# Slots' stage of a triangle and Fourier layer: x arrives with channels on partitions from the first stage's transposes, the factors' product moves to GpSimd, and the loads ahead of the triangle go

## Chip, cores and metric

The kernel runs on 1 core of one Trainium2 chip. The metric is the device time of one execution in microseconds, the median of several runs. All data is float32. The engines are TensorE (PE, with its weight loads shown as PEld), VectorE (DVE), ScalarE (ACT), GpSimd (POOL) and SyncE (SP, which only issues DMAs here).

## What is computed

x has the shape (1, 512, 512, 64): 512 rows, 512 columns, 64 channels. Two layers follow each other, each with a group normalisation in front and a residual sum behind. The reference, cut to what matters:

```python
# layer 0, on xn = _ln(_gn(x), norm_w, norm_b)
left  = (xn @ left_w  + left_b)  * mask * sigmoid(xn @ lgate_w + lgate_b)
right = (xn @ right_w + right_b) * mask * sigmoid(xn @ rgate_w + rgate_b)
out_gate = sigmoid(xn @ ogate_w + ogate_b)
out = einsum('bkjd,bkid->bijd', left, right)
x = x + (_ln(out, onorm_w, onorm_b) @ out_w + out_b) * out_gate
# layer 1: 12 x 12 Fourier modes of _gn(x), mixed over channels, and back
x = x + irfft_of_modes(einsum('bcmn,comn->bomn', fft2(_gn(x))[:12, :12], w))
```

`mask` is the outer product of a 0/1 vector of 512 entries with itself. Where it is 0 the row or column gives nothing to `left`, `right` and the einsum.

## The kernel before

With at most 256 (`K`) valid entries in the mask the branch `compact` runs, as it does with these inputs. Rows of x are ordered by rank, the valid ones first, so that the first two blocks of 128 ranks (`r` = 0 and 1) hold all valid rows; a *slot* is a valid column. Blocks 2 and 3 hold the other rows. The stages follow each other:

1. **Reading x** (L683 to L782). For each of 16 tiles `jc` of 32 columns, `fetch_tile` issues four indirect gathers of 1 MB on POOL's queue (blocks 0 and 1 into the two halves of `xg`, blocks 2 and 3 into two `yg`), two tiles ahead. PE transposes pairs of columns (128 rows by 2 x 64 channels) into banks `x_ps` of four transposes, six banks in turn (L768), and VectorE takes `bn_stats` of each bank (L769). `keep` copies the columns that are slots out of `xg` into the resident buffer `xc`: one copy for each of the 32 columns, 128 rows by 2 blocks by 64 channels, into a place whose number is a register value. Columns that are no slot go into a spare place behind the 256. ScalarE copies columns 0 to 21 (`SHARE`), GpSimd 22 to 31 (L746); the registers are filled by `slots_of` (L653) with loads of up to 16 values. `scale_weights`, `keep_weights`, `widen` and `keep_wide` put small ScalarE steps between the tiles.
2. **Scale and shift**: `group_norm_affine` joins the statistics into `ab1`.
3. **The slots' stage** (L799 to L956), 64 groups `q` of four slots, order written by hand. Per group: PE transposes the four slots so that channels lie on partitions (`turn_x`, L822; the first six groups ahead, in banks that are still free); ScalarE applies scale and shift and writes the result over `xc` (`channels`, L832); PE subtracts the mean over channels (`centered`, L843), ScalarE squares, VectorE sums (L944). For four groups at a time nine small VectorE steps (`rsqrt_steps`) make 1/sqrt; `spread` transposes these factors on PE, copies them (L862), writes them to `rs_d` in DRAM and reads them back as a broadcast to 64 partitions (L863, L869, both on POOL's queue). VectorE multiplies (`normed`, L876), PE projects twice ("gates", "sides", L882), ScalarE takes the sigmoids (L914), VectorE adds the bias and multiplies (L939), and SP stores `left_d` and `right_d`. Normalising runs 13 groups (`lead`) ahead of projecting. `early`, at the groups in `turns`, gathers x for a later stage into parts of `xc` whose slots are done, on POOL's queue. In the last four groups `load_sides` (L796) already loads seven eighths of the first four channels' `left_d` and `right_d`.
4. **The triangle** (L966 to L1016): 64 channels, each with transposes of the two sides, a product, and a store of `tri_d`.
5. The rest: the outer normalisation, gate and residual, statistics, Fourier modes, and the output. The change does not touch it.

Of the kernel before, what the change touches and what calls it, by code (L numbers as in the profile page):

```python
# [46 lines left out]
def conv_preact_kernel(ctx: ExitStack, tc: tile.TileContext, t: dict):  # L47
# [580 lines left out]
    def compact(fc):  # L628
# [20 lines left out]
        def slots_of(engine, jc, first=0, last=JC):  # L649

            regs = []
            for k in range(first, last, 16):
                _, some = nc.values_load_multi_w_load_instructions(  # L653
                    slot_row[0:1, jc * JC + k : jc * JC + min(k + 16, last)], engines=(engine,), min_val=0, max_val=K,
                    skip_runtime_bounds_check_because="a rank is not negative, and the minimum with K was taken",
                )
                regs += some
            return regs
# [23 lines left out]
        with tc.tile_pool(name="wt", bufs=1) as cp:  # L682
            with tc.tile_pool(name="f1", bufs=1) as sp, tc.tile_pool(name="f1x", bufs=2) as xp, tc.tile_pool(  # L683
# [59 lines left out]
                def keep(engine, copy, jc, first, last):  # L743

                    for j, slot in enumerate(slots_of(engine, jc, first, last), first):
                        copy(xc[:, bass.ds(slot, 1)].rearrange("p o r c -> p (o r) c"), xgs[jc][0][:, :, j, :])  # L746

                fetch_tile(0)
                fetch_tile(1)
                for jc in range(NJ):  # L750
# [10 lines left out]
                    for r in range(4):  # L761
                        flat = xgs[jc][1][r].rearrange("p j c -> p (j c)")
                        for c in range(4):

                            ps = pt.tile([P, 4, P], F32, name="x_ps")
                            for i in range(4):
                                o = (8 * c + 2 * i) * C
                                nc.tensor.transpose(ps[:, i, :], flat[:, o : o + P], ident)  # L768
                            nc.vector.bn_stats(  # L769
                                stats[:, 0, 16 * (jc % quarter) + 4 * r + c, :], ps.rearrange("p i k -> p (i k)")  # L770
                            )
# [4 lines left out]
                    keep(mybir.EngineType.Activation, nc.scalar.copy, jc, 0, SHARE)  # L776
                    keep(mybir.EngineType.Pool, nc.gpsimd.tensor_copy, jc, SHARE, JC)
# [7 lines left out]
            early_rows = 7 * P // 8  # L785

            def load_sides(c, rows=slice(0, P)):

                for k, (name, src) in enumerate((("left", left_d), ("right", right_d))):
                    if (name, c) not in raws:  # L790
                        if c < 4:
                            o = 4 * JC * 2 * C + (2 * c + k) * 2 * K
                            raws[name, c] = places[:, o : o + 2 * K].rearrange("p (b k) -> p b k", b=2)
                        else:
                            raws[name, c] = ip.tile([P, 2, K], F32, name=name + "_raw")
                    nc.sync.dma_start(raws[name, c][rows], src[c].rearrange("(p b) k -> p b k", b=2)[rows])  # L796

            rs_d = dram.tile([K // 4 // QB, 2, QB, 4 * P], F32, name="rs_d")
            with tc.tile_pool(name="fn", bufs=3) as np_, tc.tile_pool(name="fw", bufs=2) as wk, tc.tile_pool(  # L799
                name="fr", bufs=3  # L800
            ) as rp, tc.tile_pool(name="fg", bufs=1) as sp, tc.tile_pool(name="fo", bufs=5) as op, tc.tile_pool(
                name="fpt", bufs=2, space=PSUM
            ) as pt, tc.tile_pool(name="fpp", bufs=1, space=PSUM) as pp, tc.tile_pool(
                name="fpc", bufs=1, space=PSUM
            ) as pc, tc.manual_schedule():
# [3 lines left out]
                def gts(q):  # L809

                    return xc[:, 4 * q : 4 * q + 4].rearrange("p i r c -> p (i r c)")

                four = ("gates_c0", "gates_c1", "sides_c0", "sides_c1")
                turned_x = {}

                def turn_x(q):
                    if q < 2 or q > 5:
                        tps = pt.tile([P, 4, P], F32, name="xc_ps")
                    else:
                        tps = pp.tile([P, N], F32, name=four[q - 2]).rearrange("p (i k) -> p i k", i=4)  # L820
                    for i in range(4):
                        nc.tensor.transpose(tps[:, i, :], xc[:, 4 * q + i].rearrange("p r c -> p (r c)"), ident)  # L822
                    turned_x[q] = tps

                def spare(name):
                    return pc.tile([P, N], F32, name=name)

                def channels(q):
                    if q not in turned_x:
                        turn_x(q)  # L830
                    tps = turned_x.pop(q)
                    nc.scalar.activation(  # L832
                        gts(q), tps.rearrange("p i k -> p (i k)"), AF.Identity, bias=ab1[:, 1:2], scale=ab1[:, 0:1]
                    )

                def centered(q):
                    if q % 2 == 0 or q >= lead:
                        cps = spare("cc_ps")
                    else:
                        cps = spare("rc_ps") if q < 7 else pp.tile([P, N], F32, name=four[(q - 7) // 2])  # L840
                    cps = cps.rearrange("p (i c) -> p i c", c=C)
# [11 lines left out]
                def factors(k):  # L853
                    rss[k], steps = rsqrt_steps(rp, totals.pop(k), 1.0 / C, EPS, [P, QB * 8])
                    todo.extend(steps)

                def spread(k):
# [5 lines left out]
                    nc.gpsimd.dma_start(rs_d[k].rearrange("r n (i p) -> (r n i) p", p=P), turned)  # L863
                    rbs[k] = np_.tile([P, QB, N], F32, name="rbc")
# [8 lines left out]
                def normed(q):  # L873
                    k, n = divmod(q, QB)
                    xns[q] = wk.tile([P, N], F32, name="xnc")
                    nc.vector.tensor_mul(xns[q], gts(q), rbs[k][:, n])  # L876
# [15 lines left out]
                def own_of(b):  # L892
# [8 lines left out]
                    fc, sets, 2 * stats.shape[2], "xc", with_variance=lambda ab: [turn_x(q) for q in range(4)],  # L901
                    rooms=[lambda k=k: spare(k)[:, :1] for k in ("cc_ps", "rc_ps")],
                )
                turns = (11, 17, 21, 27, 33, 37)
# [3 lines left out]
                for q in range(-lead - 1, groups):  # L908
# [6 lines left out]
                    if live(1):  # L915
                        normed(q + 1)
                    some = 5 if q < 0 or q + lead >= groups else 3
                    for step in todo[:some]:
                        step()
                    del todo[:some]  # L920
                    if live(lead + 1):
                        channels(q + lead + 1)
                    early_by = 1 if q < 0 or q + lead >= groups else 0
                    if live(lead - QB + early_by) and (q + lead - QB + early_by) % QB == QB - 1:
                        k = (q + lead - QB + early_by) // QB
                        if k in rss:
                            spread(k)
# [21 lines left out]
                    if live(0):  # L949
# [5 lines left out]
                        if q >= groups - 4:  # L955
                            load_sides(q - groups + 4, slice(0, early_rows))  # L956


        with held:

            with tc.tile_pool(name="ti", bufs=5) as ip, tc.tile_pool(name="tt", bufs=3) as tp, tc.tile_pool(
# [44 lines left out]
                for c in range(4):  # L1006
                    load_sides(c, slice(early_rows, P))
# [624 lines left out]
```

## Time and profile before

| what | us |
|---|---|
| median of 3 runs | 1762.66 (1758.58 to 1766.23) |
| profiled execution: time, span | 1766.65, 1764.9 |
| reading x: first transpose of x, last slot copy on ScalarE, on GpSimd | 17.4, 194.5, 198.0 |
| first `channels` (scale and shift ready) | 200.2 |
| first gates of the slots' stage | 221.4 |
| end of the last bias and product (L939) | 433.7 |
| first transpose of a side in the triangle | 442.5 |

The busy time of the engines over the whole span is

| engine | busy us | share |
|---|---|---|
| PE | 1550.1 | 88% |
| DVE | 1410.6 | 80% |
| ACT | 949.7 | 54% |
| POOL | 933.7 | 53% |

How to read the lines that follow: a group's line names source line, engine, operation, written tile <- read tiles, shape and count, then busy time in us and mean ns of one instruction, then the idle time of the engine before them and what ended it. A timeline line gives start and length in us, merges neighbours of one kind, and shows in brackets how long the engine had been idle and what released it. A line of waits gives the total, the number and the longest.

### The profile page before, as it was taken

To read this page: it belongs to the slowest core of one execution; us is meant where nothing else is said; L and a number is where in the kernel's file an instruction comes from. 1 tells how busy PE (TensorE), PEld (TensorE's weight loads), DVE (VectorE), ACT (ScalarE), POOL (GpSimd) and SP (SyncE) were. 2 spreads that over 40 slices of the span, in tenths; PEclk is the share of its full clock that TensorE was granted. 3 is DMA by queue.
4 is the path that set the end of the run, shared out by engine and by line. 5 is a ranking of instruction groups with operands and counts; after the bars stand their busy time and mean duration, and the time that the engine had idled before them with its cause. 6 is when DMAs were issued, how large, how long until landed. Compare 5 with 4: busy or idle time off the path is not lost. (4 is left out here: it accounts for less than half of the span.)

```text
span 1764.9 us, 32756 instructions
## 1 busy us (share of the span) xinstructions
PE 1550.1 (88%) x10926; PEld 1243.5 (70%) x10926; DVE 1410.6 (80%) x2965; ACT 949.7 (54%) x1740; POOL 933.7 (53%) x695
## 2 busy tenths in 40 slices
PE   6777799997999887999999999999999868998772
PEld 5666766663899776888888888888888735665431
DVE  7999788886455568889999999999999984875551
ACT  3666677773333276777777777777777632011000
POOL 3666211110000037799999999999999881111110
PEclk9999999998999989999999999999999985555555
DMA  7999489988799789578777767776777699999998
GB/s 274 392 380 380 149 202 303 281 264 260 263 305 303 248 249 333 193 244 291 248 247 265 246 235 251 258 251 239 246 264 245 216 309 421 427 427 426 427 427 364
DMA packets 190995, 518.49 MB, mean 294 GB/s; under 512 B 38080, under 2 KB 104896, under 8 KB 147936
## 3 DMA queue, kind: packets, MB, share of 16 engines
q1 hardware_dynamic: 156528, 295.72, 48.1%
q0 software_dynamic: 30816, 218.38, 33.8%
q10 hardware_dynamic: 3472, 2.20, 0.5%
q8 instruction: 89, 1.46, 0.3%
q14 instruction: 90, 0.74, 0.1%
HBM read 311.60 MB, written 204.60 MB: 292 GB/s over the span
## 5 line engine op out<-in xcount | busy, mean ns | idle before, releaser
L1143 PE MATMUL w_ps<-gate_x,xt_c 128*128 128x128 f32 x2048 | 280.8, 281 | 30.7 <-DVE z_t L1372 29.3
L1211 POOL TENSOR_TENSOR xc<-xc,z_t 128x1024 f32<-128x1024 f32 x127 | 301.3, 2372 | 8.0
L1143 PEld LDWEIGHTS w_ps<-gate_x,xt_c 128*128 128x128 f32 x2048 | 252.5, 194 | 47.7 <-DVE z_t L1372 46.0
L1143 PE MATMUL c_ps<-center_x,xt_c 128*128 128x128 f32 x2048 | 276.5, 279 | 1.4 <-ACT xt_c L1177 0.6
L1143 PEld LDWEIGHTS c_ps<-center_x,xt_c 128*128 128x128 f32 x2048 | 252.5, 194 | 4.3 <-ACT xt_c L1138 3.1
L1538 PE MATMUL l_ps<-xc,rinv 24*128 24x512 f32 x512 | 208.0, 1136 | 30.5 <-DVE xc L1545 19.9
L1266 DVE BATCH_NORM_STATS2 stats2c<-xc 128x6 f32<-128x128 f32 x1024 | 220.4, 278 | 8.2 <-POOL xc L1211 8.2
L1181 DVE TENSOR_REDUCE scratch<-sq_c 128x16 f32<-128x1024 f32 x160 | 194.5, 1216 | 25.8 <-ACT sq_c L1176 21.4
L1376 POOL TENSOR_TENSOR z_t<-z_t,bias_row_out 128x1024 f32<-128x1024 f32 x32 | 75.7, 2365 | 254.2 <-DMA xc<-tri_d 230.0
L1319 ACT ACTIVATE z_t<-z_t 128x1024 f32<-128x1024 f32 x128 | 135.5, 1058 | 131.6 <-DVE z_t L1378 126.5
L1538 PEld LDWEIGHTS l_ps<-xc,rinv 24*128 24x128 f32 x512 | 121.1, 306 | 112.5 <-DVE xc L1545 58.4
L1138 ACT ACTIVATE xt_c<-t_ps,ab_xc 128x512 f32<-128x512 f32 x256 | 176.0, 688 | 9.0 <-PE t_ps L1136 8.2
L1372 DVE TENSOR_TENSOR z_t<-w_ps,rs_n 128x512 f32<-128x512 f32 x256 | 172.0, 672 | 6.0 <-PE w_ps L1143 5.9
L769 DVE BATCH_NORM_STATS2 stats1c<-x_ps 128x6 f32<-128x512 f32 x256 | 158.4, 684 | 13.1 <-PE x_ps L768 12.5
L1174 ACT ACTIVATE sq_c<-c_ps 128x512 f32<-128x512 f32 x256 | 150.7, 589 | 31.1 <-PE c_ps L1143 30.6
L1378 DVE TENSOR_TENSOR z_t<-z_t,scratch 128x1024 f32<-128x1024 f32 x128 | 156.3, 1221 | 10.3 <-ACT rs_n L1187 3.8
L1207 POOL TENSOR_TENSOR z_t<-z_t,xc 128x1024 f32<-128x1024 f32 x64 | 151.7, 2371 | 15.4 <-ACT z_t L1319 15.2
L1136 PE MATMUL t_ps<-c_ident,xc 128*128 128x128 f32 x1024 | 157.8, 277 | 0.0
L1545 DVE TENSOR_TENSOR xc<-xc,l_ps 128x512 f32<-128x512 f32 x176 | 109.2, 682 | 57.2 <-DMA xc<-x_h,dst_i 45.0
L1136 PEld LDWEIGHTS t_ps<-c_ident,xc 128*128 128x128 f32 x1024 | 117.9, 142 | 51.4 <-issue 51.1
L1207 POOL TENSOR_TENSOR z_t<-z_t,bias_row_out 128x1024 f32<-128x1024 f32 x63 | 149.8, 2377 | 7.3 <-ACT z_t L1319 7.0
L746 ACT COPY xc<-xg 128x128 f32 x352 | 105.0, 298 | 63.5 <-POOL xc L746 38.3
(231 smaller groups left out, 2557.8 us busy)
## 6 DMA issues: line engine op xcount, KB each, us to landing
x_h<-xc SPq DMA_DIRECT2D x64, 1024.0 KB
out_x<-xc SPq DMA_DIRECT2D x44, 1024.0 KB
xc<-u_d SPq DMA_DIRECT2D x512, 64.0 KB
out_x<-lx_t SPq DMA_DIRECT2D x20, 1024.0 KB
left_d<-o_c SPq DMA_DIRECT2D x64, 256.0 KB
right_d<-o_c SPq DMA_DIRECT2D x64, 256.0 KB
tri_d<-tri_t SPq DMA_DIRECT2D x64, 256.0 KB
xc<-tri_d SPq DMA_DIRECT2D x64, 256.0 KB
```

Of the source, the lines that this page charges most:

```text
L769: nc.vector.bn_stats(stats[:, 0, 16 * (jc % quarter) + 4 * r + c, :], ps.rearrange("p i k -> p (i k)"))
L1136: nc.tensor.transpose(tps[:, i, :], flat[:, o : o + P], ident)
L1138: nc.scalar.activation(xts[s], tps, AF.Identity, bias=ab1[:, 2:3])
L1143: nc.tensor.matmul(ps[:, 2 * i : 2 * i + 2, :], xts[s][:, i, :], w, start=True, stop=True)
L1174: nc.scalar.activation(sq, cps, AF.Square)
L1181: nc.vector.tensor_reduce(totals[k % 2][:, 8 * (n - 1) : 8 * (n + 1)], sqs.pop(s // 2), AX.X, ALU.add)
L1207: nc.gpsimd.tensor_mul(zs[k, c], zs[k, c], u)
L1211: nc.gpsimd.tensor_add(xr, xr, zs.pop((k, c)))
L1266: nc.vector.bn_stats(st[k // 4][:, g, k % 4, :], x_of(k)[:, :, 2 * g : 2 * g + 2])
L1372: nc.vector.tensor_mul(z[:, 8 * odd : 8 * odd + 8, :], wps, rs)
L1378: nc.vector.tensor_add(z, z, bias_ps["ogate"].unsqueeze(1).to_broadcast([P, 16, C]))
L1538: nc.tensor.matmul(ps.rearrange("p j o -> p (j o)"), rinv[h, b, :], it[h], start=True, stop=True, tile_position=(32 * g, 0),)
```

## The change

The slots' copies now take their data from PSUM, after the transpose, so that `xc` is filled with channels on partitions from the first stage. For that a bank must hold the two blocks r = 0 and r = 1 of one column. For odd columns this is done by a transpose of the pair (column before, column) of block 1, of which the upper half of the result is then overwritten by a transpose of block 0's column; for even columns GpSimd first copies block 1's even columns over block 0's odd ones. The banks run in the order 0, 8, 1, 9, and so on: 0 to 3 odd columns, 4 to 7 even ones, 8 to 15 blocks 2 and 3. ScalarE alone makes all 32 copies of a tile; each of the two register loads now takes every other slot number.

In the slots' stage `turn_x` and its banks are gone, and `channels` works in place on `xc`. `normed` runs on GpSimd, two groups ahead in place of one, with three buffers. The broadcast loads of the factors move out of `spread` into `fetch_factors`, issued one group later. The first results of the Newton steps lie in PSUM (`newton`), always five steps are done per group, and `spread` comes one group sooner throughout. `turns` becomes (9, 14, 20, 27, 35, 43). `load_sides` loads whole sides into buffers of the triangle stage, only after the slots' stage.

```diff
-        def slots_of(engine, jc, first=0, last=JC):
+        def slots_of(engine, jc, first=0, step=1):
...
-                def keep(engine, copy, jc, first, last):
-
-                    for j, slot in enumerate(slots_of(engine, jc, first, last), first):
-                        copy(xc[:, bass.ds(slot, 1)].rearrange("p o r c -> p (o r) c"), xgs[jc][0][:, :, j, :])
...
-                    for r in range(4):
-                        flat = xgs[jc][1][r].rearrange("p j c -> p (j c)")
-                        for c in range(4):
-
-                            ps = pt.tile([P, 4, P], F32, name="x_ps")
+                    own = xgs[jc][0]
+                    filled = 0
+                    for e in (0, 8, 1, 9, 2, 10, 3, 11, 12, 4, 13, 5, 14, 6, 15, 7):
+
+                        ps = pt.tile([P, 4, P], F32, name="x_ps")
+                        if e == 4:
+                            nc.gpsimd.tensor_copy(
+                                own[:, 0].rearrange("p (j o) c -> p j o c", o=2)[:, :, 1],
+                                own[:, 1].rearrange("p (j o) c -> p j o c", o=2)[:, :, 0],
+                            )
+                        for i in range(4):
+                            if e < 4:
+                                j = 8 * e + 2 * i + 1
+                                nc.tensor.transpose(
+                                    ps[:, i, :], own[:, 1, j - 1 : j + 1, :].rearrange("p j c -> p (j c)"), ident
+                                )
+                                nc.tensor.transpose(ps[:C, i, :], own[:, 0, j, :], ident)
+                                continue
+                            if e < 8:
+                                part = own[:, 0, 8 * (e - 4) + 2 * i :][:, :2, :]
+                            else:
+                                o = e % 4 * 8 + 2 * i
+                                part = xgs[jc][1][e // 4][:, o : o + 2, :]
+                            nc.tensor.transpose(ps[:, i, :], part.rearrange("p j c -> p (j c)"), ident)
+                        nc.vector.bn_stats(
+                            stats[:, 0, 16 * (jc % quarter) + filled, :], ps.rearrange("p i k -> p (i k)")
+                        )
+                        filled += 1
+                        if e < 8:
+                            if e % 4 == 0:
+                                slots = slots_of(mybir.EngineType.Activation, jc, 1 - e // 4, 2)
                             for i in range(4):
-                                o = (8 * c + 2 * i) * C
-                                nc.tensor.transpose(ps[:, i, :], flat[:, o : o + P], ident)
...
+                                nc.scalar.copy(
+                                    xc[:, bass.ds(slots[e % 4 * 4 + i], 1)].rearrange("p o r c -> p (o r c)"), ps[:, i, :]
+                                )
...
-                    keep(mybir.EngineType.Activation, nc.scalar.copy, jc, 0, SHARE)
-                    keep(mybir.EngineType.Pool, nc.gpsimd.tensor_copy, jc, SHARE, JC)
...
+            def load_sides(c):
+
+                for name, src in (("left", left_d), ("right", right_d)):
+                    raws[name, c] = ip.tile([P, 2, K], F32, name=name + "_raw")
+                    nc.sync.dma_start(raws[name, c], src[c].rearrange("(p b) k -> p b k", b=2))
...
                 def channels(q):
-                    if q not in turned_x:
-                        turn_x(q)
-                    tps = turned_x.pop(q)
-                    nc.scalar.activation(
-                        gts(q), tps.rearrange("p i k -> p (i k)"), AF.Identity, bias=ab1[:, 1:2], scale=ab1[:, 0:1]
-                    )
+                    nc.scalar.activation(gts(q), gts(q), AF.Identity, bias=ab1[:, 1:2], scale=ab1[:, 0:1])
...
-                    rss[k], steps = rsqrt_steps(rp, totals.pop(k), 1.0 / C, EPS, [P, QB * 8])
+                    rss[k], steps = rsqrt_steps(rp, totals.pop(k), 1.0 / C, EPS, [P, QB * 8], newton[:, k % 4])
...
+                def fetch_factors(k):
+
...
                 def normed(q):
                     k, n = divmod(q, QB)
-                    xns[q] = wk.tile([P, N], F32, name="xnc")
-                    nc.vector.tensor_mul(xns[q], gts(q), rbs[k][:, n])
+                    xns[q] = vp.tile([P, N], F32, name="xnc")
+                    nc.gpsimd.tensor_mul(xns[q], gts(q), rbs[k][:, n])
...
-                turns = (11, 17, 21, 27, 33, 37)
+                turns = (9, 14, 20, 27, 35, 43)
+                sent = []
...
-                    if live(1):
-                        normed(q + 1)
-                    some = 5 if q < 0 or q + lead >= groups else 3
-                    for step in todo[:some]:
+                    if live(2):
+                        normed(q + 2)
+                    for k in sent:
+                        fetch_factors(k)
+                    sent.clear()
+                    for step in todo[:5]:
                         step()
-                    del todo[:some]
+                    del todo[:5]
...
-                    early_by = 1 if q < 0 or q + lead >= groups else 0
-                    if live(lead - QB + early_by) and (q + lead - QB + early_by) % QB == QB - 1:
-                        k = (q + lead - QB + early_by) // QB
-                        if k in rss:
-                            spread(k)
+                    k, n = divmod(q + lead - QB + 1, QB)
+                    if n == QB - 1 and k in rss:
+                        spread(k)
+                        sent.append(k)
...
-                        if q >= groups - 4:
-                            load_sides(q - groups + 4, slice(0, early_rows))
...
                 for c in range(4):
-                    load_sides(c, slice(early_rows, P))
+                    load_sides(c)
```

## The prediction

> **What bounds the kernel now.** I read the page first, then busy time in stretches of 50 us, then timeline, waits and DMA inside the two stages that the change touches. The profiled execution took 1766.65 us (span 1764.9); the median of the runs is 1762.66, 4.0 lower. I work out a difference against the profiled one and put it on the median.
>
> Two stretches; columns: from:to and length, busy us of PE, PEld, DVE, ACT, POOL (instructions), PE clock, DMA share, GB/s:
>
> ```profile
> 100.00:150.00 50.00, 37.18 (x312) 33.67 (x311) 47.45 (x82) 33.04 (x115) 30.83 (x60) 1.00 0.99 383
> 300.00:350.00 50.00, 50.00 (x299) 30.35 (x296) 43.20 (x92) 36.66 (x63) 9.23 (x15) 1.00 0.92 294
> ```
>
> The first lies in the stage that reads x (17 to 200 us): DMA is full, VectorE nearly. The second lies in the slots' stage (200 to 434 us): PE never idles, POOL hardly works, DMA is not far from full.
>
> What paces the reading stage: ScalarE's timeline, then the waits from 50 to 190 us, then the register loads of the slot numbers.
>
> ```profile
> 99.59 7.23 ACT L746 COPY xc<-xg 128x128 f32 x22 [3.29 <-POOL xc L746]
> 110.57 7.28 ACT L746 COPY xc<-xg 128x128 f32 x22 [3.76 <-POOL xc L746]
> 117.76 0.26 ACT L711 COPY raw_sides<-made_w 128x128 f32<-128x128 f32 x1
> ```
>
> ```profile
> ACT xc L746 <- POOL xc L746: 31.1, 9, 3.8
> POOL xc L746 <- ACT xc L746: 30.4, 13, 3.3
> ```
>
> ```profile
> L653 ACTq TENSOR_LOAD <-slot_row x32: 752/898/1053, 17.3 to 184.4; - x32
> ```
>
> ScalarE's 22 copies and POOL's 10 wait for each other, tile after tile: ACT starts at 22.57, 33.41, 44.24 and so on, about 10.84 us per tile of 4 MB (four gathers of 1 MB). The gathers keep pace exactly (383 GB/s), so copies and DMA are level.
>
> What paces the slots' stage: PE's timeline over one group of four slots.
>
> ```profile
> 302.74 1.13 PE L882 MATMUL sides_c<-xnc,raw_sides 64*128 64x512 f32 x4
> 303.70 1.02 PE L882 MATMUL gates_c<-xnc,raw_gates 64*128 64x512 f32 x4
> 304.66 0.66 PE L822 MATMUL xc_ps<-c_ident,xc 128*128 128x128 f32 x4
> 305.15 1.06 PE L843 MATMUL cc_ps<-c_center,xc 128*128 128x128 f32 x8
> 306.14 1.13 PE L882 MATMUL sides_c<-xnc,raw_sides 64*128 64x512 f32 x4
> ```
>
> From start to start: sides 0.96, gates 0.96, transposes of x 0.49, centering 0.99, together 3.40 us per group with no gap.
>
> **The change, part by part.**
>
> *Copies move to ScalarE and come from PSUM.* ScalarE now does all 32 slot copies of a tile, after two loads of 16 registers. What is one copy from PSUM into a place held in a register? Below: L711 shows 0.26 us from PSUM at this size. Above: L746 from SBUF shows 0.298, and its 22 take 7.23 us, 0.329 apiece: such copies do not overlap, some 0.03 lies between them. I take 0.26 + 0.03 = 0.29 (the row with the same source), with 0.33 as the upper end. The loads took 1.02 us where they fetch 16 (the long half of the L653 row) and, in a queue that now never waits for POOL, nothing hides them: 2 x 1.02. A tile costs ScalarE 32 x 0.29 + 2.04 = 11.3, about 11.4 with its waits, against 10.84. Weights and biases that ScalarE prepared under POOL's copies now add: four scalings of 0.40, five copies 0.16 apart, four of 0.29, three that sum to 0.8: 4.4 us, say 4.2. Start as now at 22.6 (the first bank needs both gathers of the tile; the second is there at 21.2 now, and a table load of 1.28 follows); the first of the 32 loads lies before it. End of the copies: 22.6 + 16 x 11.4 - 1.0 + 4.2 = 208.2. Now the last statistics end at 194.8 and the scale and shift from them are ready at 200.2, 5.4 later; with six banks the last statistics can be about 2 us ahead of the last copy, so they are ready at 208.2 - 2 + 5.4 = 211.6: **+11.4 us**. Ends: if DMA still paces it (10.85 a tile, weights hidden), about +1; with 0.33 a copy 12.6 a tile, +31, and with 0.04 us for each of eight waits per tile (the event semaphores of ACTq took up to 0.038) 12.9, +35.
>
> The Trainium skill, "ScalarE: Activation LUTs", section "What ACT_TABLE_LOAD costs", gives 186 ns plus 0.833 ns per element, and an overlap of 93 ns between neighbours. By that an isolated copy is 293 ns, near the row's 298, but a row of them comes every 200 ns, an estimate of 6.4 + 2.0 = 8.4 us a tile: DMA would pace and the sum below would be about -22. The row's 0.329 with the place in a register contradicts the overlap, and I go by the row.
>
> PE gains 16 transposes a tile: 80 x 0.108 (16 loads of weights in 1.73 us) = 8.7 us, under 10.84; they hide behind DMA and ACT. POOL gains one copy of 1024 elements a tile: between 0.30 (128 elements, L746) and 2.37 (two inputs, below), near 1.2; it waits for PE's first four odd banks, and the four gathers of the next tile but one stand behind it on POOL's queue, then issue when PE is done with the tile. That is some 4 us earlier than now, since they no longer wait for copies; so xg and yg stay in time although the second bank already needs the third gather.
>
> *Nothing transposes x in the slots' stage.* PE: 3.40 - 0.49 = 2.91 us per group. ScalarE's channels read SBUF in place of PSUM (0.77 now); with sigmoids 1.34 and square 0.59 that is 2.70 a group, below PE's 2.91, and 0.2 more would still fit. *The product goes to POOL.*
>
> ```profile
> L876 DVE TENSOR_TENSOR xnc<-xc,rbc 128x512 f32<-128x512 f32 x64 | 43.6, 681 | 3.7 <-DMA rbc<-rs_d 3.7
> L1211 POOL TENSOR_TENSOR xc<-xc,z_t 128x1024 f32<-128x1024 f32 x127 | 301.3, 2372 | 8.0
> ```
>
> DVE now has o_c 1.41, reduction 0.68, product 0.68 and nine small steps of 0.2 in four groups: 3.2 per group; without the product 2.55. POOL: half of 2.37, 1.2 us a product; in four groups 4.8, plus issues rs_d 0.51 and rbc 1.03, and the wait for rs_d to land (up to 5.7) that the products stand behind. It stays below 11.6, and products are made two groups ahead: from rs_d's issue, landing 4.1, issue of rbc 1.0, landing 7.3 (max. 8.9) and product 1.2 sum to 13.6 against six groups, about 17, until PE needs it. Cover gone, a product on the path would cost (1.2 - 0.68) x 64 = 33 us.
>
> The Trainium skill speaks against this: "GPSIMD Engine Reference", section "4.1 Engine selection", wants elementwise work on VectorE, GpSimd being about 2 times slower with two inputs. The rows agree on the price (1.2 against 0.68); on an idle queue it is not paid, if it were the sum would be above zero.
>
> So DMA is the next limit. Its queues from 240 to 420 us (packets, MB, share):
>
> ```profile
> q1 hardware_dynamic: 8809, 28.90, 48.4%
> q0 software_dynamic: 3424, 20.53, 42.4%
> ```
>
> 53 groups in 180 us: writes 0.484 x 180 / 55 = 1.58 us a group; q0 76.3 us, less six gathers at 2.7 (reading stage), is 60 for 13 spreads of the factors, 1.16 a group. Together 2.74, with the gathers 3.05. If a packet's time is fixed, 3.05 is the floor of a group; PE's is 2.91. I take **3.05**. For the 51 groups with centering: 51 x (3.05 - 3.40) = **-17.9**. Ends: 2.91 gives -25, a floor of 3.3 (DMA never better filled than the 0.92 seen) -5.
>
> The last 13 groups took 394.8 to 433.7, 38.9 us: DVE bound (product 0.68, o_c 1.41, steps), then a stall:
>
> ```profile
> 420.05 0.69 DVE L876 TENSOR_TENSOR xnc<-xc,rbc 128x512 f32<-128x512 f32 x1 [3.71 <-DMA rbc<-rs_d]
> 442.54 5.25 PE L974 MATMUL side_ps<-c_ident,xc 128*128 128x128 f32 x24 [9.84 <-DMA xc<-left_d]
> ```
>
> Without product they are PE's: 13 x 1.95 = 25.4, the same late factors 3.7, and some 3 for the lower clock behind such a stall (0.66 in 420 to 430): 32.4, **-6.5**; ends -10 and -3.
>
> *No loads ahead of the triangle.* PE begins 8.8 us after the last o_c now, because the small remainders wait for the last writes. Whole loads wait for the same writes: landing 4, then two loads of 256 KB at 300 GB/s with 2 us of latency, 8 us; the next pair comes 1.7 later, faster than PE's 2.56 us per channel. In return 1.8 MB leave the crowded end. **+1**, between 0 and +4.
>
> Warm-up (200 to 221 us) is ScalarE's 0.77 + 0.59 per group in both: 0. Sum: 11.4 - 17.9 - 6.5 + 1 = **-12.0**, so 1762.7 - 12.0 = **1750.7**.
>
> **Rivals.**
>
> *DMA takes PE's place entirely.* For: share 0.92 to 1.0 already, o_c has five buffers, and late factors stalled DVE once. Against: writes alone reach 398 GB/s in short slices. Groups of 3.3: -5; end -3; with +11.4 and +1 the sum is +4, **1767**, within half a per cent.
>
> *Slower: ScalarE's copies become the stage's bound.* Place: the reading stage, per tile two uncovered register loads and 32 copies that never overlap. Price 16 us for each us per tile. At 12.9 us, +35 - 23.4 = +12, **1775**. It decides from 12.15 us a tile, where the loss is 23.4. For: 0.329 is the only row of such copies. Against: that row reads SBUF.
>
> *Both limits stay out of sight.* DMA paces the reading (+1), PE the groups (-25 - 8): -31, **1732**. For: the product of a fixed packet time is only supposed. Against: the loads of 1.02 are real.
>
> **How the numbers follow.** My forecast has 0.42, DMA's place 0.20, ScalarE's bound 0.25, both out of sight 0.13. Half a per cent, 8.8 us, is about what this kernel's measurement can tell from none. Faster: 0.42 x 0.83 + 0.13 = 0.48; slower: 0.25 x 0.85 + 0.2 x 0.2 = 0.25; the rest, 0.27, within. Alone, the forecast spans 1740 to 1760. To leave out no more than 2 in 10 the range must reach 1732 and 1776.
>
> **What will show it.** ACT's starts per tile in the reading stage: 11.4 right, 10.9 or 12.6 and more wrong. ScalarE's copies without POOL between, at 0.29. The scale and shift ready at 212. PE from gates to gates: 3.05, with DMA share near 1.0 and, if DMA limits, o_c waiting for left_d. No PE wait for POOL's product. PE's first side transposes 9 to 10 us after the last o_c. Behind the triangle all should be as before; a difference there makes the prediction wrong, as does a PE that waits for xnc.

## The result, and the profile after

The changed kernel takes 1841.89 us (median of 4 runs, 1839.66 to 1844.3) against 1760.62 for the one before beside it: a ratio of 1.0457, 95% interval 1.0426 to 1.0488. Forecast was 1750.7. The profiled execution has a span of 1842.5 us, 77.6 more than before. Where they lie, by the same milestones as before (us):

| | before | after | difference |
|---|---|---|---|
| start to first `channels` (scale and shift ready) | 200.2 | 286.8 | +86.6 |
| from there to the first gates | 21.2 | 21.5 | +0.3 |
| slots' stage: first gates to end of the last o_c | 212.3 | 210.4 | -1.9 |
| from there to the first transpose of a side | 8.8 | 6.3 | -2.5 |
| triangle, to the first matmul behind it | 176.1 | 175.9 | -0.2 |
| the rest | 1146.3 | 1141.6 | -4.7 |

The rest is untouched code; in the kernels that follow it took 1140.5 to 1145.3, the kernel before with other register loads among them (1142.6), so its -4.7 is scatter. So two things want explaining: a reading stage that grew by 87 us, and a slots' stage that gained nothing where 24 were forecast.

A stretch of each stage as before, reading stage and slots' stage (busy us of PE, PEld, DVE, ACT, POOL, then PE clock, DMA share, GB/s):

```profile
100.00:150.00 50.00, 38.03 (x260) 34.98 (x261) 32.61 (x54) 27.39 (x104) 15.24 (x17) 0.83 0.66 257
350.00:400.00 50.00, 46.69 (x237) 25.29 (x234) 40.63 (x80) 36.42 (x61) 26.61 (x28) 0.97 0.96 300
```

In the first, no resource is full: DMA fell from 0.99 to 0.66 and ScalarE, which now makes all copies, is busy 55% of the time. A stage in which nothing is busy waits for something that is not counted as busy. ScalarE's timeline there:

```profile
99.56 4.72 ACT L788 COPY xc<-x_ps 128x128 f32 x16 [3.34 <-issue]
104.18 0.40 ACT L698 ACTIVATE scaled_gates<-raw_gates,v_norm_w 128x128 f32<-128x128 f32 x1
107.78 4.72 ACT L788 COPY xc<-x_ps 128x128 f32 x16 [3.20 <-DVE stats1c L780]
```

Sixteen copies take 4.72 us, 0.295 each, as forecast. But 3.3 us lie ahead of every sixteen, named once "issue" and once VectorE's statistics, which had ended 0.3 us before the copies began. The register loads fill this gap (the load before the copies at 107.78 runs from 104.20 to 107.57):

```profile
L653 ACTq TENSOR_LOAD <-slot_row x32: 3366/3384/3413, 16.5 to 273.9; - x32
```

The load of 16 numbers takes 3.38 us where it took 1.02. A tile is 2 x (4.72 + 3.34) = 16.1 us. The trace of before already had a register load that costs as much a number, GpSimd's for its 10 adjacent numbers:

```profile
L653 POOLq TENSOR_LOAD <-slot_row x16: 2272/2282/2297, 18.1 to 186.9; - x16
```

That is 0.23 us a number, against 0.06 in ScalarE's load of 16.

In the slots' stage an undisturbed group is what was hoped for, from one sides to the next 3.01 us (3.40 before):

```profile
360.65 1.13 PE L877 MATMUL sides_c<-xnc,raw_sides 64*128 64x512 f32 x4
361.61 1.02 PE L877 MATMUL gates_c<-xnc,raw_gates 64*128 64x512 f32 x4
362.57 1.16 PE L835 MATMUL cc_ps<-c_center,xc 128*128 128x128 f32 x8
363.66 1.13 PE L877 MATMUL sides_c<-xnc,raw_sides 64*128 64x512 f32 x4
```

But PE, which never idled there before, now does, and takes that gain back. One place, all engines:

```profile
455.15 1.06 POOL L864 DMA_DIRECT2D rbc<-rs_d  x2 [1.56 <-DMA rs_d<-turned_c]
455.79 1.76 DVE L209 TENSOR_SCALAR rq_v<-total 128x32 f32<-128x32 f32 x1
456.22 1.28 POOL L871 TENSOR_TENSOR xnc<-xc,rbc 128x512 f32<-128x512 f32 x1
458.26 1.80 DVE L214 SCALAR_TENSOR_TENSOR rq_h<-rq_h 128x32 f32<-128x32 f32 x1
458.73 1.27 POOL L871 TENSOR_TENSOR xnc<-xc,rbc 128x512 f32<-128x512 f32 x1
460.77 1.35 PE L877 MATMUL sides_c<-xnc,raw_sides 64*128 64x512 f32 x3 [2.15 <-DVE o_c L935]
460.81 1.34 ACT L909 ACTIVATE sigc<-gates_c,b_all 128x512 f32<-128x512 f32 x2 [3.68 <-DVE o_c L935]
```

VectorE's step L209 on 32 elements a partition, 0.174 us before, takes 1.76 and ends at 457.55, when GpSimd's product ends (457.50); L214 takes 1.80 beside the next product. o_c stands behind these steps, and PE and ScalarE wait for it. Ten of the chain's steps take over 0.4 us in this stage, and all ten end 0.04 to 0.06 us after a product ends; those of 2.6 to 3.1 us last through two products, one right behind the other. Later, products are late as well:

```profile
507.67 1.69 PE L877 MATMUL gates_c<-xnc,raw_gates 64*128 64x512 f32 x4 [2.99 <-POOL xnc L871]
```

### The profile page after: what moved, and what is told of

It reads as the page before. It is cut to its first block, busy times and chain, and to the rows that moved or that the text cites. A ratio compares the mean times of both kernels' runs of the same rounds, so it can differ in the third digit from the quotient of the medians.

```text
span 1842.5 us, 32889 instructions
## 1 busy us (share of the span) xinstructions
PE 1591.3 (86%) x10926; PEld 1274.7 (69%) x10926; DVE 1402.0 (76%) x2901; ACT 981.5 (53%) x1900; POOL 984.4 (53%) x615
## 5 line engine op out<-in xcount | busy, mean ns | idle before, releaser
L780 DVE BATCH_NORM_STATS2 stats1c<-x_ps 128x6 f32<-128x512 f32 x256 | 164.5, 689 | 88.5 <-PE x_ps L772 76.0
L1175 DVE TENSOR_REDUCE scratch<-sq_c 128x16 f32<-128x1024 f32 x160 | 194.6, 1216 | 24.7 <-DMA xc<-tri_d 11.4
L788 ACT COPY xc<-x_ps 128x128 f32 x512 | 135.8, 265 | 118.9 <-DVE stats1c L780 63.3
```

What stands on the lines that cost most here:

```text
L780: nc.vector.bn_stats(stats[:, 0, 16 * (jc % quarter) + filled, :], ps.rearrange("p i k -> p (i k)"))
L1175: nc.vector.tensor_reduce(totals[k % 2][:, 8 * (n - 1) : 8 * (n + 1)], sqs.pop(s // 2), AX.X, ALU.add)
```

## The experiments

Each ran beside the kernel before. Medians, ratio to it with its 95% interval, and the slots' stage (first gates to end of the last o_c) of the profiled execution. The first four rows change the changed kernel; each of the last four is "contiguous and small steps" with one thing more:

| | median us | ratio | slots' stage us |
|---|---|---|---|
| contiguous slot loads | 1770.03 | 1.0062 [1.0038, 1.0086] | 197.6 |
| product on VectorE | 1838.25 | 1.0445 [1.0419, 1.047] | 200.8 |
| small steps with one SBUF input | 1834.19 | 1.0414 [1.0386, 1.0442] | 198.3 |
| loads ahead again | 1843.02 | 1.0485 [1.0449, 1.0521] | 200.1 |
| contiguous and small steps | 1757.19 | 0.9973 [0.9963, 0.9984] | 191.9 |
| that, and one load of 32 | 1756.93 | 0.9967 [0.9955, 0.9978] | 194.2 |
| that, and no early gathers | 1751.34 | 0.9942 [0.9923, 0.996] | 187.1 |
| that, and SyncE reads the factors | 1749.14 | 0.9931 [0.9915, 0.9947] | 185.7 |
| SyncE reads the factors, again | 1751.34 | 0.9938 [0.9917, 0.9959] | 187.0 |

### Contiguous slot loads

`slot_row` is written with the even numbers of a tile ahead of the odd ones, so that each load takes 16 adjacent numbers. Nothing else changes.

```diff
-        nc.vector.tensor_scalar(slot_row, row_ps, float(K), None, ALU.min)
+        nc.vector.tensor_scalar(slot_row.rearrange("o (t p j) -> o t p j", p=2, j=JC // 2),
+            row_ps.rearrange("o (t j p) -> o t p j", p=2, j=JC // 2), float(K), None, ALU.min)
...
-    slots = slots_of(mybir.EngineType.Activation, jc, 1 - e // 4, 2)
+    slots = half_of(mybir.EngineType.Activation, jc, 1 - e // 4)
```

> The changed kernel with one thing undone: the row of slot numbers is stored even columns first, odd columns behind, tile by tile, so that ScalarE's two loads per tile keep their number, size and place but read 16 neighbours in place of every other number (SP's loads read both halves). Theory (the stride of the register loads is the loss): a load falls from 3.38 to about 1.02 us, a tile from 16.2 to 32 x 0.295 + 2 x 1.02 = 11.5 us, the reading stage ends about 75 us sooner, median 1842 - 75 = 1767. Rival (the load is long because of where it stands, behind copies that read PSUM and in front of a wait for PE): loads stay at 3.4, tile 16, median 1842. Second rival (six banks and ScalarE's place in the ring set the tile): loads 1.0, but the tile stays above 14, median above 1805.

Its register loads, and its ScalarE timeline:

```profile
L655 ACTq TENSOR_LOAD <-slot_row x32: 1012/1022/1047, 17.1 to 204.3; - x32
```

```profile
108.28 4.72 ACT L791 COPY xc<-x_ps 128x128 f32 x16 [0.84 <-DVE stats1c L783]
113.98 4.72 ACT L791 COPY xc<-x_ps 128x128 f32 x16 [0.98 <-DVE stats1c L783]
119.68 4.72 ACT L791 COPY xc<-x_ps 128x128 f32 x16 [0.98 <-DVE stats1c L783]
```

The load is back at 1.02, the gap at 0.98, a tile at 11.4, and scale and shift are ready at 214.8 us, 72.0 sooner. The median fell by 72 too: the stride is most of the loss, shown by taking away nothing else.

### What a number costs that is not adjacent

Two kernels change the loads alone: in the kernel before, ScalarE's 22 numbers come in two loads of 11 that take every other one; in the changed kernel, each load of 16 with stride 2 becomes two of 8 with stride 4. A third fills all 32 registers with one contiguous load (with the small steps below).

```diff
-    slot_row[0:1, jc * JC + k : jc * JC + min(k + 16, last)]
+    slot_row[0:1, jc * JC + k : jc * JC + min(k + 16 * step, last) : step]
...
-    slots = slots_of(mybir.EngineType.Activation, jc, 1 - e // 4, 2)
+    pairs = [slots_of(mybir.EngineType.Activation, jc, 1 - e // 4 + 2 * h, 4) for h in range(2)]
+    slots = [reg for pair in zip(*pairs) for reg in pair]
```

> The kernel before, where only ScalarE's register loads change: its 22 slot numbers of a tile come in two loads of 11 that take every other number, in place of 16 and 6 adjacent ones. Theory (a number that is not adjacent costs 0.21 us, and in this kernel the loads lie in the 3.6 us a tile in which ScalarE waits for GpSimd's copies): each load 2.3 us, 4.6 a tile in place of 1.8, of which 3.6 are covered; a tile 7.23 + 4.6 = 11.9 in place of 10.84, 16 x 1.05 = 17 us, median 1777, between 1770 and 1785. Rival (nothing is covered, 2.8 a tile lie on the path): 1805. Third (all covered): 1762.

> The changed kernel, but each load of 16 with stride 2 becomes two loads of 8 with stride 4. Theory (every number that is not adjacent to the one before is read by itself, 0.21 us each, whatever the distance): a load of 8 takes 1.7 us, 6.8 a tile as before, time within 5 us of 1842. Rival (the cost goes with the bytes spanned): 3.4 us a load, 13.5 a tile, 1842 + 16 x 6.8 = 1950. Third (each load has a large fixed part): between, by its size.

> As e5, but ScalarE fills its 32 registers of a tile with one contiguous load in place of two of 16. Theory (a load costs a fixed part and a small part for each register: 0.76 us for 6 and 1.02 for 16 give 0.60 + 0.026 each): the load takes 1.44 us, a tile 9.44 + 1.44 + 0.1 = 11.0 in place of 11.4, 16 x 0.5 = 8 us less than e5, or some 9 at most, where the gathers' 10.84 a tile is the floor. Rival (a load costs 0.064 us a register): the load takes 2.04, the tile stays at 11.4, e5's time within 3 us.

ScalarE's loads in these three kernels, in this order, min/median/max in ns:

```profile
L654 ACTq TENSOR_LOAD <-slot_row x32: 2331/2346/2373, 16.5 to 200.4; - x32
```

```profile
L653 ACTq TENSOR_LOAD <-slot_row x64: 1712/1718/1802, 16.6 to 282.2; - x64
```

```profile
L655 ACTq TENSOR_LOAD <-slot_row x16: 1949/1966/1995, 16.9 to 198.5; - x16
```

8, 11 and 16 numbers that are not adjacent take 1.72, 2.35 and 3.38 us: 0.21 each, at a stride of 2 and of 4. 16 and 32 adjacent ones take 1.02 and 1.97 on ScalarE, 0.06 each. Adjacency alone isn't the whole rule: GpSimd's 10 adjacent numbers cost 0.23 each. They start at column 22 of a tile, ScalarE's loads at column 0 or 16; whether the engine or the place makes the difference was not tried. The fixed part that the expectation read out of 0.76 for six numbers doesn't carry over; the load of 32 saves 0.07 us a tile and its median equals that of its parent. The load with stride 4 ran at 1846.36 (one run), as its theory had it.

The kernel before with strided loads took 1778.63 us, 1.0096 times the original [1.0075, 1.0117]. Its ScalarE timeline shows how much of the price it had covered:

```profile
107.33 7.23 ACT L748 COPY xc<-xg 128x128 f32 x22 [4.56 <-issue]
119.26 5.91 ACT L748 COPY xc<-xg 128x128 f32 x18 [4.70 <-issue]
```

A tile is 7.23 + 2 x 2.35 = 11.93. The loads grew by 4.7 - 1.8 = 2.9 us a tile, the tile by 1.09: the rest went into the time in which ScalarE had waited for GpSimd's copies. The change took that cover away and made the loads dearer, both at once.

### The small steps behind the product

Product back on VectorE:

```diff
-    nc.gpsimd.tensor_mul(xns[q], gts(q), rbs[k][:, n])
+    nc.vector.tensor_mul(xns[q], gts(q), rbs[k][:, n])
```

> The changed kernel with one thing undone: the factors' product runs on VectorE again (two groups ahead as in the change). Theory (VectorE's small steps that read two inputs from SBUF, or use both its ports, stand still while GpSimd runs its product or a DMA issue): the first step of the Newton chain (max 3.08 us now) and the fifth (max 2.89) fall to 0.18 and 0.19 everywhere; VectorE then carries 3.2 us a group, so the slots' stage from first gates to last bias, 210 us now, becomes 200 to 212; median 1832 to 1844. Rival (the small steps are long because of semaphores or DMA traffic): their maxima stay near 3 us, and the stage grows by VectorE's 0.68 a group to about 230, median 1860.

Product on GpSimd, but every small step reads at most one operand from SBUF and has another operand or its result in PSUM; that costs one step more (ten in place of nine), and `prepare` runs 12 groups sooner:

```diff
-    rss[k], steps = rsqrt_steps(rp, totals.pop(k), 1.0 / C, EPS, [P, QB * 8], newton[:, k % 4])
+    rss[k], steps = one_in_sbuf(rp, totals.pop(k), 1.0 / C, EPS, [P, QB * 8], *(newton[:, i + k % 4] for i in (0, 4, 8)))
```

> The changed kernel, product still on GpSimd, but no small VectorE step has two inputs in SBUF or an SBUF input with an SBUF output of a one-input step: intermediate values alternate between PSUM and SBUF (ten steps in place of nine), and the six preparing steps move from the first six projecting groups to the warm-up, before the products begin. Theory (shared port): the long steps vanish, groups stay at the undisturbed 3.0 us throughout, the slots' stage goes from 210 to about 51 x 3.03 + 35 = 190, median about 1822. Rival (stalls come from waits, not ports): steps stay long, median 1842 or above it by the tenth step. Second rival (DMA is the floor behind them): steps short, but the groups fill up with waits for stores or factors, stage above 200, median above 1833.

The steps in the changed kernel, then the same step with its result in PSUM:

```profile
L209 DVE TENSOR_SCALAR rq_v<-total x16: 181/182/3080, 295.8 to 484.9; 128x32 f32<-128x32 f32 x16
L210 DVE TENSOR_SCALAR newton<-rq_v x16: 194/195/196, 296.0 to 485.1; 128x32 int32<-128x32 int32 x16
```

```profile
L850 DVE TENSOR_SCALAR newton<-total x16: 194/195/195, 296.3 to 473.2; 128x32 f32<-128x32 f32 x16
```

L209 reads and writes SBUF and takes up to 3.08 us; L210, which writes PSUM, never more than 0.196. With no GpSimd product, or with PSUM in every step, no step is stalled (none is above 0.2 us). GpSimd's DMA issues alone don't stall them: with the product on VectorE 15 of the L209 and L214 steps ran beside one, none longer than 0.193. The Trainium skill, "GPSIMD Engine Reference", section "1. Specifications", says that GpSimd shares its SBUF interfaces with VectorE, with contention for VectorE instructions in a 2-port mode or with two SBUF inputs. L214, which reads two SBUF inputs, agrees, and stalled up to 2.89 us; L209 has one input and would fit only in a 2-port mode, which no row here names.

In time, each of the two edits gave only 4 to 8 us (medians): something else limited the stage too. The stage's length in one profile is a weak witness while steps stall, since it depends on how the steps meet the products. In the changed kernel 10 of the 144 steps stall and lose 16.8 us in sum; with the loads ahead (below), where only the stage's last four groups differ, it is 9 steps and 8.3 us, and a stage of 200.1 in place of 210.4. The profiled execution with contiguous loads, stage 197.6, was also the fastest of its five, 1759.3 against a median of 1770.03. By the medians the small steps' edit gave 7.7 us on the changed kernel and 12.8 on contiguous loads (1770.03 to 1757.19).

### The loads ahead of the triangle

> The changed kernel with one thing undone: seven eighths of the first four channels' sides are loaded during the last four groups again. Theory (the loads ahead crowd the end of the slots' stage and their remainders wait for the last stores anyway): from the last bias to PE's first transpose of a side 8 to 9 us in place of 6.3, nothing gained behind it, median +2, about 1844. Rival (they hide the loads): 3 to 4 us in place of 6.3, median 1839.

With `load_sides` of before put back into the last four groups (and the remaining eighths behind), PE begins 10.0 us after the last o_c, not 6.3, and the median is 1843.02. The loads ahead bought nothing.

### What else holds the slots' stage

> Both edits of the contiguous slot loads and of the small steps with one SBUF input, in the changed kernel. Theory (the stride costs 72 us in the reading stage, VectorE's stalled small steps another 8 in the slots' stage, and the two add): median 1841.9 - 72 - 8 = 1762, between 1755 and 1767, no VectorE small step above 0.4 us, slots' stage (first gates to end of last product of o_c) 197 to 201 us against 210.4. Rival (the small steps stall beside a limit that paces the stage anyway, the 8 us were scatter): 1768 to 1774, stage 205 or more.

Both edits together: 1757.19, faster than the kernel before, stage 191.9. The waits from 240 to 425 us that are left in it (total, times, longest):

```profile
POOL rbc L884 <- DMA rs_d<-turned_c: 27.4, 13, 5.4
PEld gates_c L897 <- POOL xnc L891: 15.8, 18, 3.2
PE gates_c L897 <- POOL xnc L891: 6.1, 6, 2.4
```

GpSimd's queue stands 2 us for each block of factors until rs_d has landed, with the next products behind it, and PE waits for those. Two edits tell this from my forecast's floor, the DMA: leave out the stage's six gathers (`early`; a later stage then lacks these rows, so this is an experiment only), or let SyncE issue the broadcast loads.

```diff
-    if q in turns:
-        early(turns.index(q))
...
-    nc.gpsimd.dma_start(
+    nc.sync.dma_start(
         flat[h, o], rs_d[k, r].rearrange("n k -> (n k)")[o].unsqueeze(0).to_broadcast([C, o.stop - o.start])
     )
```

> As e5, but the six gathers of 1 MB that the slots' stage issues for a later stage are left out. Theory (DMA paces the groups, about 3.05 us each, six gathers at 2.7 us of the queues): the slots' stage is 10 to 16 us shorter than e5's, median 10 to 16 lower, DMA share in the middle of the stage not below 0.9 and groups at 2.9 to 2.95. Rival (the factors' way, rs_d landing, rbc issued behind it on GpSimd's queue, product, paces the stage): 0 to 6 us shorter, DMA share down to some 0.85.

> As e5, but the broadcast loads rbc are issued by SyncE, so that the products on GpSimd no longer stand behind a wait for rs_d to land. Theory (DMA paces the groups): slots' stage within 3 us of e5's, median within 4, the DMA share in it the same. Rival (the wait for rs_d on GpSimd's queue makes products late and PE wait): stage 6 to 15 us shorter, PE's waits for xnc gone. Third (rbc now holds SyncE's stores while it waits): o_c waits for left_d or right_d, the stage longer by 3 or more.

Without the gathers the stage is 4.8 us shorter and the median 5.9 lower, with SyncE 6.2 and 8.1, or 4.9 and 5.9 when run again. Both shorten the same wait. Without the gathers GpSimd's wait for rs_d fell from 27.4 to 17.7 us, and that of PE's weight loads (PEld) for the products from 15.8 to 8.8; with SyncE the latter is 3.2, or 5.9 when run again. From 300 to 350 us, first without the gathers, then with SyncE (the second run):

```profile
300.00:350.00 50.00, 50.00 (x273) 27.99 (x274) 40.45 (x93) 42.54 (x71) 27.12 (x29) 1.00 0.90 261
```

```profile
300.00:350.00 50.00, 50.00 (x274) 28.00 (x273) 40.49 (x93) 42.49 (x71) 26.20 (x24) 1.00 0.97 307
```

Equal PE work in equal time at a DMA share of 0.90 and 0.97: DMA isn't the floor, PE is, at 3.0 us a group. With neither edit PE was busy 47.45 of these 50 us at a DMA share of 0.94. By these waits, what the stage had lost lay at the head of GpSimd's queue.

### The product's place, SyncE for both transfers, and a second rhythm

All on top of the kernel in which SyncE reads the factors: the product on VectorE; one load of 32 and rs_d written by SyncE too; the parent itself and the product on VectorE once more, side by side; and one of the next tile's gathers issued in mid-tile.

> As the run in which SyncE reads the factors (median 1749.1, stage 185.7), but the factors' product is on VectorE again. Theory (moving the product is what lets PE set the pace: VectorE would need 1.50 + 0.66 + 0.68 + 10 x 0.19 / 4 = 3.3 us a group against PE's 3.0): 51 x 0.3 = 15 us more, stage 198 to 203, median 1762 to 1767, VectorE over 0.95 busy. Rival (VectorE has room, the place of the product is worth nothing): within 3 us of 1749.

> As the run in which SyncE reads the factors, with one load of 32 in place of two of 16, and SyncE writes rs_d too. Theory (PE paces the groups at 3.0 and what is left is outside GpSimd's queue): within 3 us of 1749, stage 183 to 187, the reading stage 1 us shorter at most, since 32 numbers took 1.97 us and twice 16 took 2.04. Rival (SyncE's wait for ScalarE's copy of the factors holds the stores): stage 190 or more, o_c waits for left_d or right_d.

> The same kernel as the run in which SyncE reads the factors (1749.1), beside the one with the product on VectorE. In the last two runs the reading stage, whose instructions are the same, took 13.7 us a tile in place of 11.4, with TensorE's clock at 0.85 to 0.9 in place of 1.0. Theory (the rhythm of this stage has two cycles, and which one comes hangs on the chip or on chance, not on the edits of the slots' stage): both kernels of this call show the same tile, 11.4 or 13.7; this one 1749 or 1785. Rival (an edit of the slots' stage or the load of 32 brings it): 1749 here with 11.4, and 13.7 in the other.

> The same kernel as the one with the product back on VectorE (1793.7). Theory of the two cycles: the same tile as the other kernel of this call, and behind the reading stage the same slots' stage as before, some 196 us against 186, 8 to 10 us more than the run beside it. Rival: 1794 while the run beside it has 1749.

> As the run in which SyncE reads the factors, but of the four gathers of the next tile but one the one of block 2 is issued in the middle of a tile, as soon as PE is done with its buffer, not with the others at the end. Theory (the slow cycle starts where the DMA queues run empty, PE idles for some us, its clock falls, its transposes free the buffers late and the queues run empty again; a gather in stock breaks it): 11.4 a tile and 1746 to 1750 whichever cycle the others show, DMA share nowhere below 0.85 between 40 and 190 us. Rival (the clock falls for another reason): the same tile as the kernel it comes from.

The first two took 1793.7 and 1790.53 us, far above either expectation. Their slots' stages, 194.4 and 197.0, explain only some 10 us of it; 30 us lie in the reading stage. From 100 to 150 us, the product on VectorE, then its parent run again:

```profile
100.00:150.00 50.00, 43.55 (x330) 41.32 (x331) 39.50 (x66) 32.47 (x125) 17.43 (x19) 0.87 0.77 298
```

```profile
100.00:150.00 50.00, 42.28 (x359) 38.56 (x357) 44.96 (x76) 38.28 (x147) 19.31 (x20) 1.00 0.96 377
```

The stage's instructions are the same, and it took 13.7 us a tile with PE at a clock of 0.87 and DMA at 0.77. Run once more beside its parent on another chip, the product on VectorE took 1761.33 us (0.9996 [0.9984, 1.0008]) with 11.4 a tile, and the parent 1751.34. So the reading stage has two rhythms, and the place of the product, an edit of the later stage, doesn't choose between them. The kernel before took its usual 1762.78 beside the runs with the long one.

With that set aside: the product on VectorE makes the slots' stage 194.3 us against 187.0, and the median 10 us longer: the move to GpSimd is worth 10 us, once its queue no longer waits. SyncE writing rs_d as well made the stage 197.0: its rival's case, o_c waiting 7.6 us in all for right_d, whose stores stand behind the wait for ScalarE's copy of the factors.

The early gather failed: 1772.09 us (1.0061 [1.0046, 1.0075]). Its tiles from the second to the sixth took 11.4 to 11.7 us, those from the seventh on 13.5 to 14.3, in one execution and with PE's clock at 1.00:

```profile
100.00:150.00 50.00, 37.27 (x302) 32.09 (x301) 39.23 (x65) 31.96 (x123) 17.09 (x18) 1.00 0.83 306
```

So tiles of 13.5 us come without a low clock, and a gather in stock doesn't prevent them: my account of how they start isn't borne out. This edit changes the reading stage itself, so whether its slow tiles are the same rhythm isn't shown. What starts the long rhythm, and whether the chip decides, stays open.

## Why the prediction was wrong, by its own steps

- **The register loads: the step that failed.** "The loads took 1.02 us where they fetch 16" was taken from loads of adjacent numbers; after the change each load takes every other number, and that access had no row in the trace of before. It should have had bounds from both sides, and the upper one stood beside it: GpSimd's 0.23 us a number, 3.6 us for 16. Measured: 3.38. 32 loads x (3.38 - 1.02) = 75.5 us. With the forecast's +11.4 this gives 86.9 for the reading stage, and 86.6 was measured, but so close by luck: with the stride taken away the stage was 72.0 us shorter, and what was left cost 14.6, not 11.4. The Trainium skill has a figure near the measured one: "Runtime: NRT & Kernel Launch", section "🔬 Instruction fetch mechanics", puts a register load at about 200 ns a register even in bulk. It speaks of loads from HBM; here, on ScalarE and from SBUF, 0.21 was measured for numbers not adjacent and 0.06 for 16 or 32 adjacent ones. By its figure a load of 16 would be an estimate of 3.2 us.
- **The copies.** 0.29 forecast, 0.295 measured; the cadence of 200 ns, an estimate worked out from the Trainium skill's "ScalarE: Activation LUTs", section "What ACT_TABLE_LOAD costs", didn't come. With adjacent loads scale and shift came at 214.8, forecast 211.6.
- **The rival with ScalarE as the bound** had the right place and mechanism ("two uncovered register loads"), and the price too low: 12.9 us a tile as the upper end, 16.1 measured. Its upper end rested on the same 1.02.
- **Slots' stage, -17.9 and -6.5.** It gave -1.9. PE's group is 3.01, not 2.91: from start to start centering takes 1.09 us, not 0.99. Its weight loads now wait up to 0.8 us for ScalarE's square, which may be the reason; that wasn't tested. The floor of 3.05 was right in size by luck, since its cause is wrong: DMA isn't the limit. What took back the gain weren't terms of the sum at all: VectorE's steps, 0.2 us each by their rows, stalled up to 3.1 us beside GpSimd's products; and the products waited for rs_d and rbc, a wait that the forecast named and thought covered by six groups, about 17 us. Its sum for GpSimd in four groups didn't cover the longest wait: 4.8 + 0.51 + 1.03 + 5.7 is 12.0, not below 11.6. With both mended and SyncE's queue for rbc the stage gains 25.3 to 26.6 (212.3 to 187.0 and 185.7), near the forecast's 24.4.
- **Loads ahead, +1.** The gap before the triangle shrank by 2.5 us. Sign wrong, small.
- **Warm-up 0, POOL's product 1.2:** 0.3 and 1.277 measured.

So the change is good for 0.6 to 0.7% once three things are mended: the order of the slot numbers, the operands of the small steps, and the queue of the factors' loads. That version is faster than both kernels, 1749 to 1751 us, where the reading stage keeps its short rhythm.

## What to carry to other kernels

Price an instruction by a row with the same access pattern, not only the same name and count: a stride in a slice is another operation. In a stretch where no engine is busy, look at what is not counted as busy (register loads, waits at the head of a queue), and don't trust the releaser named if it was done before. When work moves to an idle engine, ask what it shares (the SBUF interface with VectorE) and what already waits in its queue.

## What the runs showed of the hardware that was not expected

- A register load from SBUF on ScalarE takes 0.21 us for each number not adjacent to the last (8: 1.72, 11: 2.35, 16: 3.38), and 0.06 for 16 or 32 adjacent ones (1.02, 1.97); 6 adjacent ones took 0.76, and 10 on GpSimd 2.28.
- A VectorE step of 0.18 us with input and output in SBUF takes up to 3.1 us beside GpSimd's two-input products of 1.277 us, until one of them ends; a step that writes PSUM keeps its 0.195.
- The same reading stage ran at 11.4 or 13.7 us a tile in different runs of one kernel, with PE's clock at 1.00 or 0.87. What decides it is open.
